# Moving a runtime loop ahead of the last sequence's normalisation in a fused attention and mixture-of-experts kernel

## The chip, the cores and the metric

The kernel runs on one core of one Trainium2 chip. Such a core has five engines that run side by side [...]: TensorE (PE in the profile; its weight loads are PEld), VectorE (DVE), ScalarE (ACT), GpSimd (POOL) and SyncE (SP), which here only issues transfers. Sixteen DMA engines move the data. The metric is device time in microseconds (us), the median of several runs; lower is better. Before the change the median of three runs is 1431.23 us (1428.58 to 1433.54).

## The reference

The input x holds 8 sequences of 512 rows of 256 numbers, all in float32. Two layers follow, each normalised on the way in and on the way out and added to its input:

```python
x = x + _layernorm(_L0_attn_ref(_layernorm(x, axis=-1), wq, bq, wkv, bkv, wo), axis=-1)
x = x + _layernorm(_L0_ffn_ref(_layernorm(x, axis=-1), gate_w, w_gate, w_up, w_down,
                               sh_gate, sh_up, sh_down), axis=-1)
```

The first is causal attention with 16 query heads of 128 that share 4 key and value heads, with a position code added to queries and keys. The second is a mixture of experts, plus a shared feed-forward part that every row passes:

```python
scores = jax.nn.softmax(logits, axis=-1)             # 64 experts
topk_w, topk_idx = jax.lax.top_k(scores, TOP_K)      # 6 of them for each row
...
pos = jnp.arange(T * TOP_K) - starts[eid_s]
valid = pos < CAP                                    # an expert takes its first 64 rows
...
y = jnp.einsum('tkh,tk->th', out_exp.reshape(T, TOP_K, H), topk_w)
y = y + gs * us @ sh_down.T                          # the shared part
```

T is here the 8 x 512 = 4096 rows of all sequences, so an expert's 64 places are filled in the order of the rows, and most experts are full long before the last rows come.

## The kernel before, in words

The kernel is written with a layer that places semaphores itself. For nearly the whole kernel the order of each engine's instructions is the order of the program text (a block that is opened with `tc.manual_schedule` for all five engines and closed with `order.close()`, L1015).

**Attention** goes through 8 x 16 heads in a software pipeline (the loop over k). The feed-forward steps of the sequence before are spread over the heads of the next, by a table of steps and places in `feed_forward`.

**Experts.** They are handled in 32 pairs. The first five sequences (`EARLY`) fill nearly all places; their rows are gathered, passed through the 32 pairs and scattered. Pairs that still have free places afterwards are listed in the tile `work`: its first number is the count of such pairs less one, and the numbers behind it name them. The first of these pairs, called "late", is worked out within the main order for sequences 5, 6 and 7: its weights are loaded beforehand, and each sequence gathers its rows by a product with a 0/1 matrix (`gather`), computes the pair (`gate_up`, `gate_up_hidden`, `turn_hidden`, `down`), and adds the result to its own sums with one more matmul in the PSUM banks of the sums.

**The other pairs** with free places, if there are any, are the business of the loop at L1019, `with tc.For_i(0, table["rest"], 1)`. Its count is only known on the chip. Its body reads back from device memory what the sequences 5, 6 and 7 left for it (scores and places in `lxg_d`, sums in `ly_d`, the rows x1 in `x1_d`), computes one pair, adds it to `ly_d`, normalises the rows again and writes them to the output again. In the kernel before, the loop is the last thing in the program. The trace holds no instruction of its body: with these inputs the count is zero. Every engine still goes through its gate, whose instructions carry the line L1019; the program's closing instructions carry L1094.

**The last part** (`last_part`, L837) is sequence 7's feed-forward, which has no further head to hide behind. In it,

- `other` and `output6` stand for sequence 6, whose feed-forward is finished here too. `output6()` advances the steps of `output` (L645): the first takes the statistics of the sums (VectorE, with a power on POOL), the second scales them (ACT) and adds x1 (POOL), the third issues the store of 512 KB to the output (SP, L655).
- `f` is the generator `shared` (L678) for sequence 7. It works through three chunks of the shared part; of the six steps, every second one is the hidden rows of a chunk, two VectorE instructions (L721, L722). The last `next(f)` is that of chunk 0.
- `l["part"](py, n)` adds the down product of chunk n to the sums `py` in two PSUM banks (L687), eight matmuls with their weight loads.
- the matmuls at L903 add the late pair's result, and then come sequence 7's statistics (`norm_scales`, L72), a copy of the sums by ACT that is stored to `ly_d` (L908, L909), subtraction of the mean (L911), the scaled sum with x1 (L913) and two stores of 256 KB to the output (L916).
- L872 stores sequence 7's x1 rows to `x1_d`. Only the loop's body would read these, as it would `ly_d`.

Of the kernel before, what the change touches and what calls it, by code (L numbers as in the profile page):

```python
# [16 lines left out]
ALU = mybir.AluOpType  # L17
AX = mybir.AxisListType

P = 128  # L20
B, T, E = 8, 512, 256
NT = B * T
NI = T // P
# [16 lines left out]
EARLY = 5  # L40
ET_ROWS = EARLY * T
# [3 lines left out]
def sandwich_kernel(ctx, tc, x, wq, bq_t, wkv, bk_t, bv, wo, gate_wt, w_gate, w_up, w_down,  # L45
                    sh_gate_t, sh_up_t, sh_down_t, pe_t, out):
    nc = tc.nc
# [14 lines left out]
    x1_d = dram.tile([NT, E], F32, tag="x1_d", name="x1_d")  # L62
# [3 lines left out]
    ly_d = dram.tile([NT - ET_ROWS, E], F32, tag="ly_d", name="ly_d")  # L66
# [5 lines left out]
    def norm_scales(tiles, name):  # L72

        n = len(tiles)
        st = small.tile([P, n, 6], F32, tag="st", name=f"st_{name}")
        for i in range(n):
            nc.vector.bn_stats(st[:, i, :], tiles[i])
        return scales_of(st, n, name)
# [23 lines left out]
    def rows_of(d, first):  # L102
        return d[first : first + T, :].rearrange("(i p) e -> p i e", p=P)
# [19 lines left out]
    with ExitStack() as part:  # L123
# [4 lines left out]
        p1 = pool("p1", 1)  # L128
        p2 = pool("p2", 2)
# [3 lines left out]
        ET = mybir.EngineType  # L133
# [28 lines left out]
        for half, (t, w) in enumerate(((sg_sb, sh_gate_t), (su_sb, sh_up_t))):  # L162
            nc.sync.dma_start(out=t[:, :, :FSH], in_=w.rearrange("(c p) n -> p c n", p=P))
            nc.sync.dma_start(out=t[:, :, FSH:],
                              in_=gate_wt.rearrange("(c p) n -> p c n", p=P)[:, :, ts(half, NX // 2)])
# [389 lines left out]
        def gate_up_hidden(key):  # L555
            l = pairs[key]
            pgu = l.pop("pgu")
            nc.vector.scalar_tensor_tensor(l["hid"], l["hid"], 1.0, pgu[:, 0, :], ALU.add, ALU.mult)
            nc.vector.scalar_tensor_tensor(l["hid"], l["hid"], 0.5, pgu[:, 1, :], ALU.mult, ALU.mult)

        def turn_hidden(key):
            l = pairs[key]
            pt = ps_s.tile([P, 2, P], F32, tag="s", name=f"pth_{key}")
            cols = l["hid"].rearrange("s (p c) -> s c p", c=2)
            for c in range(2):
                nc.tensor.transpose(pt[:FC, c, :], cols[:, c, :], ident)  # L566
            l["ht"] = p3.tile([FC, 2, P], F32, tag="ht", name=f"ht_{key}")
            on_dve(l["ht"], pt[:FC])
# [268 lines left out]
        def last_part(before, spare):  # L837


            b, xt, sums = B - 1, seqs[B - 1]["x"], po.pop(B - 1)  # L840
            l = {}
            other, shared6, output6 = before["l"], before["shared"], before["output"]
            for _ in spare:
                pass
            shared6()
            mv, rs = norm_scales([sums[i // 2][:, i % 2, :] for i in range(NI)], f"o{b}")
            next(other["f"])
            two = p2.tile([P, 2, NI * E], F32, tag="v", name="o_xt2")
            o, xt2 = two[:, 0].rearrange("p (i e) -> p i e", i=NI), two[:, 1].rearrange("p (c t) -> p c t", c=NC)
            st = small.tile([P, NI, 6], F32, tag="st", name=f"st_f{b}")  # L850

            for i in range(NI):
                nc.vector.scalar_tensor_tensor(xt[:, i, :], sums[i // 2][:, i % 2, :], rs[:, i : i + 1], xt[:, i, :],
                                               ALU.mult, ALU.add)
                nc.vector.bn_stats(st[:, i, :], xt[:, i, :])
            shift = shifts(mv, rs, f"o{b}")
            py6 = [ps_o.tile([P, 2, E], F32, tag=f"o{n}", name=f"py_{b - 1}_{n}") for n in range(2)]
            other["part"](py6, 2)
            mv, rs = scales_of(st, NI, f"f{b}")
            other["hidden"](0)  # L860
            fshift = shifts(mv, rs, f"f{b}")
            xg = p1.tile([P, NI, ROW], F32, tag="xg", name=f"xg_{b}")
            for i in range(NI):
                if i % 2:
                    scale_on_act(xg[:, i, :E], xt[:, i, :], rs, fshift, i)
                else:
                    normalize(xg[:, i, :E], xt[:, i, :], mv, rs, i)
            other["hidden"](1)
            transpose_rows(xt2, xg, f"f{b}")
            for i in range(NI):  # L870
                nc.gpsimd.tensor_scalar(xt[:, i, :], xt[:, i, :], shift[:, i : i + 1], 1.0, ALU.add, ALU.mult)
            nc.sync.dma_start(out=rows_of(x1_d, b * T), in_=xt)  # L872
            other["part"](py6, 0)
            f = shared(b, xt2, l, "msmsms")
            next(f)
            other["part"](py6, 1)
            r = route(b, xg, l)
            next(r)
            other["late"](py6)
            next(r)  # L880
            next(r)
            next(f)
            next(f)
            next(r)
            marked = marks(table["m"], xg[:, :, E:ROW], table["places"], b, p2, "xnt")
            next(f)
            next(f)
            gather("late", [(xg, marked[0])])
            gt = turn_scores(marked[1], b, p2, "kt", 5)
            gate_up("late")  # L890
            next(f)
            py = l["py"] = [ps_o.tile([P, 2, E], F32, tag=f"o{n}", name=f"py_{b}_{n}") for n in range(2)]
            l["part"](py, 2)
            l["part"](py, 1)
            gate_up_hidden("late")
            turn_hidden("late")
            l["part"](py, 0)
            down("late")
            output6()
            output6()  # L900
            output6()
            for i in range(NI):
                nc.tensor.matmul(py[i // 2][:, i % 2, :], lhsT=gt[:, ts(i, P)], rhs=pairs["late"]["dd"],  # L903
                                 start=False, stop=True, skip_group_check=True)
            mv, rs = norm_scales([py[i // 2][:, i % 2, :] for i in range(NI)], f"y{b}")
            y = p2.tile([P, NI, E], F32, tag="xnt", name=f"y_{b}")
            for n in range(2):
                nc.scalar.copy(y[:, ts(n, 2), :], py[n])  # L908
            nc.sync.dma_start(out=rows_of(ly_d, b * T - ET_ROWS), in_=y)  # L909
            for i in range(NI):  # L910
                nc.vector.tensor_scalar(o[:, i, :], py[i // 2][:, i % 2, :], mv[:, i, 0:1], None, ALU.subtract)  # L911
            for i in range(NI):
                nc.vector.scalar_tensor_tensor(xt[:, i, :], o[:, i, :], rs[:, i : i + 1], xt[:, i, :],  # L913
                                               ALU.mult, ALU.add)
                if i % 2:
                    nc.sync.dma_start(out=rows_of(out, b * T)[:, i - 1 : i + 1, :], in_=xt[:, i - 1 : i + 1, :])  # L916

        EARLY_TAGS = [(p3, "wgu"), (p3, "wd")]

# [91 lines left out]
        turned_at_once(NK - 1)  # L1011
        mix(NK - 1)
        project(NK - 1)
        last_part(behind, routed)
        order.close()  # L1015


# [1 line left out]
        with tc.For_i(0, table["rest"], 1) as n:  # L1019
            m = nc.values_load(table["work"][0:1, ds(n + 2, 1)], (ET.DVE, ET.SP), min_val=0, max_val=NM - 1)  # L1020
            pairs["late"] = {"m": m}
            load_gate_up("late")
            load_down("late")
            parts, gts = [], []
            for b in range(EARLY, B):
                q, tag = [(p1, "hid"), (p2, "v"), (p2, "v")][b - EARLY]
                xg = q.tile([P, NI, LROW], F32, tag=tag, name=f"rest_xg_{b}")
                nc.sync.dma_start(out=xg, in_=rows_of(lxg_d, b * T - ET_ROWS))
                q, tag = [(p1, "y"), (p2, "x"), (p2, "x")][b - EARLY]
                mark, marked = marks(m, xg[:, :, E:ROW], xg[:, :, ROW:], f"rest_{b}", q, tag)  # L1030
                parts.append((xg, mark))
                gts.append(turn_scores(marked, f"rest_{b}", p2, "kt", 5))
            gather("late", parts)
            gate_up("late")
            gate_up_hidden("late")
            turn_hidden("late")
            down("late")
            for b in range(EARLY, B):
                y = p2.tile([P, NI, E], F32, tag="xnt", name=f"rest_y_{b}")
                nc.sync.dma_start(out=y, in_=rows_of(ly_d, b * T - ET_ROWS))  # L1040
                for i in range(NI):
                    py = ps_m.tile([P, E], F32, tag="m", name=f"rest_py_{b}_{i}")
                    nc.tensor.matmul(py, lhsT=gts[b - EARLY][:, ts(i, P)], rhs=pairs["late"]["dd"], start=True, stop=True)
                    nc.vector.tensor_add(y[:, i, :], y[:, i, :], py)
                nc.sync.dma_start(out=rows_of(ly_d, b * T - ET_ROWS), in_=y)
                for _ in output(b, y, residual(b, p1, "xn")):
                    pass


# [48 lines left out]
```

## Time and profile before

| What | us |
|---|---|
| median of three runs | 1431.23 (1428.58 to 1433.54) |
| the profiled execution, its own time | 1433.63 |
| the profiled execution, span from first to last instruction | 1431.9 |
| PE busy in the span | 1393.9 |
| DVE busy | 888.9 |
| ACT busy | 505.3 |
| POOL busy | 428.9 |

The profile is that of one execution. Its page gives each engine's busy time, the share of every fortieth of the span, the DMA queues, the chain of work that ended last (followed back from the last instruction to whatever released it), and groups of instructions with the number of executions, the busy time and the mean duration. Waits, branches and the issue of transfers belong to an engine's sequencer (a q behind the engine's name) and aren't counted as busy. An L with a number is a line of the kernel, and a tile's name is that in the text without its number: `py` at L903 is `py_7`, the sums of sequence 7. Times within the trace are counted from the first instruction.

### The profile page before, as it was taken

To read this page: it belongs to the slowest core of one execution; us is meant where nothing else is said; L and a number is where in the kernel's file an instruction comes from. 1 tells how busy PE (TensorE), PEld (TensorE's weight loads), DVE (VectorE), ACT (ScalarE), POOL (GpSimd) and SP (SyncE) were. 2 spreads that over 40 slices of the span, in tenths; PEclk is the share of its full clock that TensorE was granted. 3 is DMA by queue.
4 is the path that set the end of the run, shared out by engine and by line. 5 is a ranking of instruction groups with operands and counts; after the bars stand their busy time and mean duration, and the time that the engine had idled before them with its cause. 6 is when DMAs were issued, how large, how long until landed. Compare 5 with 4: busy or idle time off the path is not lost.

```text
span 1431.9 us, 18567 instructions
## 1 busy us (share of the span) xinstructions
PE 1393.9 (97%) x5310; PEld 850.3 (59%) x5310; DVE 888.9 (62%) x3097; ACT 505.3 (35%) x1442; POOL 428.9 (30%) x686
## 2 busy tenths in 40 slices
PE   9999999999999999999999999999999999999895
PEld 5666665666656665656556665655556555556563
DVE  5565576656765576656765577566666545577634
ACT  2333333234422343234422343233443333444421
POOL 2231242113311232123211232124544344444311
PEclk9999999999999999999999999999999999999998
DMA  7765565356554564356544564358998789778702
GB/s 239 206 199 142 146 174 162 110 132 171 168 144 124 147 185 136 99 156 168 161 127 128 162 195 129 99 155 275 308 286 250 227 232 264 201 235 265 234 15 82
DMA packets 160791, 252.03 MB, mean 176 GB/s; under 512 B 16412, under 2 KB 136189, under 8 KB 160685
## 3 DMA queue, kind: packets, MB, share of 16 engines
q1 hardware_dynamic: 125869, 201.52, 48.4%
q10 hardware_dynamic: 28672, 39.85, 9.0%
q0 software_dynamic: 6144, 9.44, 3.3%
q8 instruction: 43, 0.70, 0.2%
q14 instruction: 63, 0.52, 0.1%
HBM read 143.01 MB, written 107.74 MB: 175 GB/s over the span
## 4 chain that ended last, share of the span: by engine, by line
PE 83%; DVE 8%; DMA 2%; ACT 2%; issue 2%; POOL 1%; SPq 0%; DVEq 0%; ACTq 0%; POOLq 0%
PE pav L349 17%; PE psc L289 16%; PE po L361 13%; PE pq L276 13%; PE pk L248 4%; PE pv L259 4%; PE psg L708 3%; PE psu L708 3%; PE pgu L549 2%; PE py L735 2%; DVE eb L322 2%; PE pd L575 2%; ACT e L296 2%; DMA ex_d<-eb 1%; PE pth L566 1%
## 5 line engine op out<-in xcount | busy, mean ns | idle before, releaser
L306 POOL TENSOR_SCALAR e<-e,recip 128x128 f32<-128x128 f32 x508 | 269.7, 571 | 775.3 <-DVE recip L303 762.4
L296 ACT ACTIVATE e<-e,least 128x128 f32<-128x128 f32 (+3 forms) x512 | 285.7, 559 | 350.4 <-DVE least L293 332.6
L289 PE MATMUL psc<-kt,qt 128*128 128x128 f32 (+3 forms) x1024 | 307.7, 438 | 9.9 <-DVE least L293 3.5
L349 PE MATMUL pav<-et,v 128*128 128x512 f32 (+3 forms) x1024 | 297.1, 433 | 1.4 <-DMA et<-ex_d 1.1
L349 PEld LDWEIGHTS pav<-et,v 128*128 128x128 f32 x1024 | 193.6, 190 | 161.0 <-issue 113.8
L293 DVE CUSTOM_DVE_ANT_0 e<-psc,mask 128x128 f32<-128x128 f32 (+3 forms) x512 | 232.2, 479 | 58.1 <-PE psc L289 52.2
L361 PE MATMUL po<-wo_sb,ao 128*128 128x256 f32 x1024 | 245.0, 383 | 0.7 <-ACT ao L109 0.7
L276 PE MATMUL pq<-xnt,wq_sb 128*128 128x512 f32 x512 | 240.9, 593 | 0.3 <-ACT sc L388 0.3
L361 PEld LDWEIGHTS po<-wo_sb,ao 128*128 128x128 f32 x1024 | 194.2, 191 | 72.5 <-issue 40.3
L109 ACT COPY ao<-pav 128x512 f32<-128x512 f32 x128 | 75.0, 586 | 435.8 <-PE pav L349 407.3
L322 DVE STREAM_TRANSPOSE eb<-e 128x128 f32<-128x128 f32 x756 | 227.5, 365 | 0.8 <-DMA ex_d<-eb 0.4
L289 PEld LDWEIGHTS psc<-kt,qt 128*128 128x128 f32 x1024 | 165.4, 190 | 85.3 <-DVE least L293 23.5
L279 DVE SCALAR_TENSOR_TENSOR qt<-pq,bq_sb,pe_sb 128x512 f32<-128x512 f32 x128 | 95.7, 748 | 106.0 <-PE pq L276 104.9
L276 PEld LDWEIGHTS pq<-xnt,wq_sb 128*128 128x128 f32 x512 | 95.9, 190 | 69.9 <-issue 64.0
L303 DVE RECIPROCAL recip<-total 128x4 f32<-128x4 f32 x128 | 22.8, 178 | 119.8 <-ACT e L296 119.8
L296 ACT ACTIVATION_READ_ACCUMULATOR e<-e,least 128x1 f32 x512 | 95.6, 187 | 0.0
L586 POOL DMA_INDIRECT y_d<-dd,idx x32 | 51.0, 1592 | 94.3 <-DMA y_d<-dd,idx 33.2
L248 PE MATMUL pk<-xnt,wkv_sb 128*128 128x512 f32 x128 | 60.3, 594 | 0.2 <-ACT xnt L109 0.2
L261 DVE TENSOR_TENSOR v<-pv,bv_sb 128x512 f32<-128x512 f32 x32 | 22.1, 691 | 60.8 <-PE pv L259 60.8
L259 PE MATMUL pv<-wkv_sb,xnt 128*128 128x512 f32 x128 | 59.1, 593 | 0.0
L251 DVE SCALAR_TENSOR_TENSOR kt<-pk,bk_sb,pe_sb 128x512 f32<-128x512 f32 x32 | 24.0, 750 | 47.5 <-PE pk L248 47.5
L112 DVE COPY ht<-pth 88x256 f32<-88x256 f32 x32 | 13.4, 418 | 55.2 <-PE pth L566 52.5
(197 smaller groups left out, 1113.6 us busy)
## 6 DMA issues: line engine op xcount, KB each, us to landing
ex_d<-eb SPq DMA_DIRECT2D x504, 160.0 KB
et<-ex_d SPq DMA_DIRECT2D x126, 640.0 KB
wgu<-in_w_gate ACTq DMA_DIRECT2D x32, 352.0 KB
wgu<-in_w_up ACTq DMA_DIRECT2D x32, 352.0 KB
wd<-in_w_down ACTq DMA_DIRECT2D x32, 352.0 KB
y<-y_d ACTq DMA_DIRECT2D x10, 512.0 KB
x<-in_x SPq DMA_DIRECT2D x8, 512.0 KB
x_d<-x SPq DMA_DIRECT2D x8, 512.0 KB
```

The lines of the kernel that those rows point to most:

```text
L248: nc.tensor.matmul(pk, lhsT=wkv_sb[:, c, g, 0, :], rhs=s["xnt"][:, c, :], start=c == 0, stop=c == NC - 1)
L259: nc.tensor.matmul(pv, lhsT=s["xnt"][:, c, ts(i, P)], rhs=wkv_sb[:, c, :, 1, :], start=c == 0, stop=c == NC - 1)
L276: nc.tensor.matmul(pq, lhsT=wq_sb[h // QPG][:, c, ts(h % QPG, D)], rhs=seqs[b]["xnt"][:, c, :], start=c == 0, stop=c == NC - 1)
L279: nc.vector.scalar_tensor_tensor(qt, pq, bq_sb[:, h : h + 1], pe_sb, ALU.add, ALU.add)
L289: nc.tensor.matmul(psc[:, :w], lhsT=l["qt"][:, ts(i, P)], rhs=seqs[b]["kt"][h // QPG][:, :w], start=True, stop=True)
L293: nc.vector.tensor_tensor_reduce(out=e, in0=psc[:, :w], in1=mask[:, T - w :], scale=-1.0 / math.sqrt(D), scalar=BIG, op0=ALU.add, op1=ALU. ...
L296: nc.scalar.activation(e, e, AF.Exp, bias=l["least"][:, i : i + 1], scale=-1.0, accum_out=l["total"][:, i : i + 1])
L306: engine.tensor_scalar(e, e, recip[:, n : n + 1], 1.0, ALU.mult, ALU.mult)
L322: nc.vector.transpose(blocks.rearrange("p c j t -> p j c t"), l["e"][i][:, js[0] * P : (js[-1] + 1) * P].rearrange("p (j c t) -> p j c t", ...
L349: nc.tensor.matmul(pav[:, :, j:, :], lhsT=seqs[b]["v"][:, j, ts(g, D)], rhs=l["et"][:, :, AT[j] : AT[j] + NI - j, :], start=j == 0, stop=j ...
L361: nc.tensor.matmul(po[b][i // 2][:, i % 2, :], lhsT=ao[:, ts(i, P)], rhs=wo_sb[:, h, :], start=h == 0 and i % 2 == 0, stop=h == NH - 1, sk ...
L708: nc.tensor.matmul(pp[:mw, :], lhsT=w_sb[:, c, ds(f0, mw)], rhs=xt2[:, c, :], start=c == 0, stop=c == NC - 1)
```

## The change

Three things are edited.

1. In `last_part`, sequence 6's three output steps, which stood together behind the last `down("late")`, are spread: the first behind `gate_up("late")`, the second behind `next(f)`, the third behind `l["part"](py, 0)`. The last `next(f)` moves from ahead of the products of chunks 2 and 1 to behind `gate_up_hidden`.
2. The loop moves ahead of the last rows' normalisation. `last_part` now ends with the matmuls at L903 and returns the sums in their banks and the x1 rows in their tile. The normalisation becomes a function of its own, `last_output`, called after the loop in a new block with a fixed order. The store of x1 (L872) and the copy and store of sequence 7's sums (L908, L909) go.
3. In the loop's body, sequence 7 is treated differently from 5 and 6: its share of a pair is added by matmuls to the banks that still hold its sums, and its rows aren't normalised there. One tile of the body changes its place (`x` becomes `xt2`).

```diff
-            nc.sync.dma_start(out=rows_of(x1_d, b * T), in_=xt)
             other["part"](py6, 0)
...
             gate_up("late")
-            next(f)
+            output6()
             py = l["py"] = [ps_o.tile([P, 2, E], F32, tag=f"o{n}", name=f"py_{b}_{n}") for n in range(2)]
             l["part"](py, 2)
             l["part"](py, 1)
             gate_up_hidden("late")
+            next(f)
+            output6()
             turn_hidden("late")
             l["part"](py, 0)
+            output6()
             down("late")
-            output6()
-            output6()
-            output6()
             for i in range(NI):
                 nc.tensor.matmul(py[i // 2][:, i % 2, :], lhsT=gt[:, ts(i, P)], rhs=pairs["late"]["dd"],
                                  start=False, stop=True, skip_group_check=True)
+            return py, xt
+
+        def last_output(py, x1):
+            b = B - 1
             mv, rs = norm_scales([py[i // 2][:, i % 2, :] for i in range(NI)], f"y{b}")
             y = p2.tile([P, NI, E], F32, tag="xnt", name=f"y_{b}")
-            for n in range(2):
-                nc.scalar.copy(y[:, ts(n, 2), :], py[n])
-            nc.sync.dma_start(out=rows_of(ly_d, b * T - ET_ROWS), in_=y)
-            for i in range(NI):
-                nc.vector.tensor_scalar(o[:, i, :], py[i // 2][:, i % 2, :], mv[:, i, 0:1], None, ALU.subtract)
-            for i in range(NI):
-                nc.vector.scalar_tensor_tensor(xt[:, i, :], o[:, i, :], rs[:, i : i + 1], xt[:, i, :],
-                                               ALU.mult, ALU.add)
+            for i in range(NI):
+                nc.vector.tensor_scalar(y[:, i, :], py[i // 2][:, i % 2, :], mv[:, i, 0:1], None, ALU.subtract)
+            for i in range(NI):
+                nc.vector.scalar_tensor_tensor(x1[:, i, :], y[:, i, :], rs[:, i : i + 1], x1[:, i, :], ALU.mult, ALU.add)
                 if i % 2:
-                    nc.sync.dma_start(out=rows_of(out, b * T)[:, i - 1 : i + 1, :], in_=xt[:, i - 1 : i + 1, :])
+                    nc.sync.dma_start(out=rows_of(out, b * T)[:, i - 1 : i + 1, :], in_=x1[:, i - 1 : i + 1, :])
...
-        last_part(behind, routed)
+        sums, x1_last = last_part(behind, routed)
         order.close()
...
-                q, tag = [(p1, "y"), (p2, "x"), (p2, "x")][b - EARLY]
+                q, tag = [(p1, "y"), (p2, "x"), (p1, "xt2")][b - EARLY]
...
-            for b in range(EARLY, B):
+            for i in range(NI):
+                nc.tensor.matmul(sums[i // 2][:, i % 2, :], lhsT=gts[-1][:, ts(i, P)], rhs=pairs["late"]["dd"],
+                                 start=False, stop=True, skip_group_check=True)
+            for b in range(EARLY, B - 1):
...
+        with tc.manual_schedule(engines={ET.PE, ET.DVE, ET.Activation, ET.Pool, ET.SP}):
+            last_output(sums, x1_last)
```

## The prediction

> **What bounds the kernel now.** I read the page first: the chain that ended last is TensorE for most of its length, so only what shortens the end of that chain can be gained. Then I asked for busy time in stretches of the last 47 us, because everything that the change touches lies there.
>
> ```profile
> span 1431.9 us, 18567 instructions
> PE 83%; DVE 8%; DMA 2%; ACT 2%; issue 2%; POOL 1%; SPq 0%; DVEq 0%; ACTq 0%; POOLq 0%
> ```
>
> ```profile
> 1396.00:1407.25 11.25, 11.07 (x59) 6.03 (x57) 9.38 (x31) 2.41 (x5) 0.00 (x0) 1.00 0.35 118
> 1407.25:1416.40 9.15, 8.61 (x42) 6.51 (x42) 3.81 (x16) 2.28 (x6) 1.92 (x3) 1.00 0.00 0
> 1416.40:1421.00 4.60, 0.00 (x0) 0.00 (x0) 4.41 (x15) 1.44 (x3) 2.84 (x4) 0.93 0.40 136
> 1421.00:1425.10 4.10, 0.00 (x0) 0.00 (x0) 0.00 (x0) 0.00 (x0) 0.00 (x0) 0.50 0.71 241
> 1425.10:1431.90 6.80, 0.00 (x0) 0.00 (x0) 0.00 (x0) 0.00 (x0) 0.00 (x0) 0.50 0.00 1
> ```
>
> The columns are stretch, its length, busy time of PE, PEld, DVE, ACT, POOL, then clock, DMA share, GB/s. TensorE is full until 1416.4; VectorE normalises the last sequence until 1421; DMA alone works until 1425.1; then nothing works for 6.8 us, and even DMA is silent. What fills them is in the view of the program's last line, for POOL, and of the loop's line, for SP and VectorE (duration min/median/max in ns, then first and last start):
>
> ```profile
> L1094 POOLq DRAIN  x3: 46/103/5302, 1425.7 to 1431.6; - x3
> L1019 SPq EVENT_SEMAPHORE  x21: 17/27/28, 1422.0 to 1426.6; - x21
> L1019 DVEq EVENT_SEMAPHORE  x14: 21/50/50, 1421.0 to 1425.5; - x14
> L1019 DVEq COMPARE_BRANCH  x3: 47/51/61, 1419.4 to 1425.6; - x3
> ```
>
> No instruction of the loop's body is in the trace: it runs zero times. But each engine executes its gate: a branch, a wait for its own work, then on leaving a dozen waits for all other engines and all DMA queues. The last of these is passed only when the last output rows have landed (1425.1), and only then, at 1425.7, does POOL reach the program's closing DRAIN, which takes 5.3 us. From its end to the end of the span are 0.8 us. So the chain ends: rows landed, gate 0.65, DRAIN 5.3, closing 0.8. The timeline shows the rows before that:
>
> ```profile
> 1415.50 1.62 DVE L77 BATCH_NORM_STATS2 st_y<-py 128x6 f32<-128x256 f32 x4 [0.77 <-PE py L903]
> ...
> 1417.52 1.65 DVE L911 TENSOR_SCALAR o_xt<-py,mv_y 128x256 f32<-128x256 f32 x4
> 1418.22 1.01 POOL L87 TENSOR_TENSOR rs_y<-ve_y,mhalf 128x4 f32<-128x4 f32 x1
> 1418.29 0.38 SPq L655 DMA_DIRECT2D out_dram<-x  x1
> 1418.71 0.51 SPq L909 DMA_DIRECT2D ly_d<-y  x1
> 1419.27 1.67 DVE L913 SCALAR_TENSOR_TENSOR x<-o_xt,rs_y,x 128x256 f32<-128x256 f32 x4
> 1420.18 1.62 SPq L916 DMA_DIRECT2D out_dram<-x  x2
> ```
>
> [...] Four engines here agree (7 to 17 ns), POOL's first does not: 5302 ns, against 170 ns for its DRAIN at the start of the program. [...] Here each engine's jump over the body took 0.4 to 0.6 us to its next instruction, with no instruction fetch inside it[...]. [...] from issue to last landing 128 KB of places took 1.95 us, 512 KB alone 2.9 to 3.0.
>
> **The change, part by part.**
>
> *Output of sequence 6, moved up between the PE blocks.* Its first step (four BATCH_NORM_STATS2, 1.39 us, aggregation and sum to 1.9) goes on VectorE from 1405.8 to 1407.65, right after the copy of gathered rows. Then the hidden rows of the pair (0.7, to 1408.4; their tanh is ready at 1407.62 anyway), and the last hidden chunk (1.4, to 1409.8), moved behind. Who waits for these? TensorE's transpose of the hidden rows at 1410.7 to 1410.9, after 3.65 us of py matmuls: 1.1 us of cover. That transpose also takes the bank that the moved chunk's second operand holds until 1409.8; same cover. If it were gone, TensorE would slip one to one. POOL's power runs at 1407.8 to 1408.8, VectorE's shift at 1409.8, ACT's four scalings (2.08) 1410.05 to 1412.1, ahead of ACT's copy of dd at 1413.9: 1.8 us of cover. POOL's four sums (2.77) end at 1413.5, and SP issues the 512 KB of output there instead of 1418.29; it lands 2.99 us later, at 1416.5 (as measured). TensorE keeps its end, 1416.35. Cost nothing.
>
> *Removed.* The store of x1 (512 KB at 1387, off every chain), two ACT copies of py (1.04) and the 512 KB store to ly_d. They are off VectorE's chain too, but DMA pays: before, three blocks drained back to back from 1419.3 to 1424, and the last 256 KB took 4.1 us from issue to landing.
>
> *The gate moved ahead of the last normalisation.* This is the cost. VectorE's first statistic needs only py, at 1415.5; now it needs every engine and landing. TensorE's own part is over at 1416.4. SP adds up eight DMA queues in order, 0.07 us each. Without the x1 store the early output sits on the first of these, landing at 1416.5, and VectorE follows with some eight more waits at 0.1 us, branch and start 0.3. Like before (landing 1425.07, three queues later VectorE past it at 1425.83), this gives a start at 1417.75. Were the landing a little earlier, TensorE is last and the start is 1416.85. The bounds are thus 1.35 and 2.25 us of delay[...]. I take 1.9, as the two releasers are within 0.15 us: start 1417.4. Behind it wait VectorE's 13 instructions, POOL's power and SP's two stores.
>
> *The last normalisation.* Before, 5.44 us from first statistic to last sum. The wait for the second py bank between statistics (0.18) is over by then; POOL's power no longer queues behind sums of sequence 6 (it started 0.6 us after its input), but the four subtractions (1.65) cover it in both. So 5.26: VectorE ends at 1422.66, SP issues at 1422.7, and 256 KB on a nearly idle queue land after about 2.3 us (an estimate between the 1.95 and 2.9 above): 1425.0. That is where it was: 1.9 lost at the gate, 2.0 regained.
>
> *The close.* POOL's last work is now its power, ending 3.1 us after the first statistic: 1420.5. Nothing stands between it and its closing DRAIN, which before carried no wait. At 5.3 us it runs 1420.6 to 1425.9, beside the last sums and stores, not after them. SP's closing wait passes at about 1425.4, so POOL's DRAIN is last, by half a microsecond. Plus 0.8: 1426.7. The sum: gate +1.9, bank wait -0.2, landing -1.8, gate at the end -0.65 with DRAIN hidden behind the landing -4.4 (of 5.3, 0.9 sticks out): -5.15 us in the profiled execution, whose span was 1431.9 and own time 1433.63 (1.7 lie around it). The median of the runs is 1431.23, 2.4 under that execution, a difference elsewhere; so 1431.23 - 5.15 = 1426.1. The DRAIN's length at its new place is not shown: from 0.17 to 5.3 us. At the short end SP's landing is last and the gain is 5.6, so only half a microsecond hangs on it. I take 5.3.
>
> **Rivals.**
> - *A fetch stall or late gate.* [...] sequence 6's rows land late. Each microsecond moves everything after. Against: no stall before. [...]
> - *The DRAIN stays last* (the slower side). If its 5.3 us wait for something at the program's end, or POOL must first wait for the last landing, then the gate is a loss with nothing to set against it but the shorter landing: 1425.0 + 0.65 + 5.3 + 0.8 = 1431.8, and with the gate's upper bound and a straggling DMA engine as before (the last 0.5 us of 1425.07) 1432.6. In the runs' terms 1431.1 to 1432.0, say 1431.6, slightly slower. It decides from a gate delay of 2 us on; over 0.3% slower needs over 6. For it: the length is unexplained. Against: before, DRAIN carried no wait and DMA was silent under it.
> - *The loop does run, or the edit does nothing*: same inputs, zero iterations before; hardly.
>
> **How the numbers follow.** Forecast 0.81, own range 1424.5 to 1427.7; fetch or gate 0.08; DRAIN last 0.10; rest 0.01. What a measurement of this kernel can tell from no change is about 0.3%, 4.3 us: below 1426.9 is faster, above 1435.5 slower. The forecast gives 0.75 of its 0.81 to faster, 0.06 to same; fetch or gate is same (0.08); DRAIN last 0.06 same, 0.04 slower, rest slower. Range 1423.4 to 1430.4: it holds the forecast with the runs' spread (2.5 us each way) and the stall, and leaves out most of DRAIN last.
>
> **What would show it.** VectorE's first statistic of py near 1417.4, behind the loop's waits; sequence 6's output issued near 1413.5; TensorE's end unmoved at 1416.4; no ly_d store there; POOL's long DRAIN starting some 0.1 us after its last power, not after the last landing; the end 0.8 us after it. Wrong if the DRAIN still starts or ends after the landing by 5 us, if TensorE's block slips, or if a jump takes over 1 us.

## The result and the profile after

The changed kernel takes 0.9972 of the time of the kernel before, with an interval of 0.9962 to 0.9983: some 4.0 us less (2.4 to 5.4). The medians of 22 runs each are 1429.98 and 1433.19 us, 3.2 us apart; the three runs from which the prediction reckoned lay 2 us under the longer series. The effect is clear of no change, and just short of the 0.3% that the prediction drew as its line.

The time went where the forecast had it go. Here are the stretches of the changed kernel that answer to those shown of before; the columns are again stretch, length, busy time of PE, PEld, DVE, ACT and POOL, clock, DMA share and GB/s. Everything up to the last sums runs 3.3 us later in this execution than in the profiled one of before, for reasons that lie earlier in the kernel (the copy of the late pair's rows starts at 1408.68 instead of 1405.37).

```profile
1410.56:1419.71 9.15, 8.62 (x44) 6.53 (x42) 2.76 (x10) 2.77 (x6) 3.78 (x5) 1.00 0.17 59
1419.71:1421.48 1.77, 0.00 (x0) 0.00 (x0) 0.00 (x0) 0.00 (x0) 0.00 (x0) 1.00 0.04 9
1421.48:1426.55 5.07, 0.00 (x0) 0.00 (x0) 5.01 (x17) 0.00 (x0) 1.02 (x1) 0.74 0.01 3
1426.55:1428.75 2.20, 0.00 (x0) 0.00 (x0) 0.00 (x0) 0.00 (x0) 0.00 (x0) 0.50 0.70 238
1428.75:1430.70 1.95, 0.00 (x0) 0.00 (x0) 0.00 (x0) 0.00 (x0) 0.00 (x0) 0.50 0.00 0
```

A new hole of 1.8 us has opened behind TensorE's end (1419.7), in which no engine works: the gate of the loop. The transfer behind the last sums has shrunk from 4.1 to 2.2 us, and the dead end, in which neither engines nor DMA work, from 6.8 to 1.95. The timeline shows the same in single steps (a bracket gives the engine's idle time before the instruction and what ended it), and the views of the loop's and of the closing instructions show who holds whom (durations in ns, then first and last start):

```profile
1416.63 0.38 SPq L655 DMA_DIRECT2D out_dram<-x  x1
...
1417.65 1.99 PE L902 MATMUL py<-dd_late,gt 128*128 128x256 f32 x8 [0.47 <-ACTq L1019]
1421.48 1.43 DVE L77 BATCH_NORM_STATS2 st_y<-py 128x6 f32<-128x256 f32 x4 [6.59 <-SPq L1019]
...
1423.30 1.65 DVE L911 TENSOR_SCALAR y<-py,mv_y 128x256 f32<-128x256 f32 x4
1423.47 1.02 POOL L87 TENSOR_TENSOR rs_y<-ve_y,mhalf 128x4 f32<-128x4 f32 x1 [6.87 <-DVE ve_y L85]
1424.87 1.66 DVE L913 SCALAR_TENSOR_TENSOR x<-y,rs_y,x 128x256 f32<-128x256 f32 x4
1425.77 1.16 SPq L915 DMA_DIRECT2D out_dram<-x  x2
```

```profile
L1019 DVEq EVENT_SEMAPHORE  x14: 21/50/50, 1414.9 to 1421.2; - x14
L1099 POOLq DRAIN  x3: 46/109/6380, 1423.4 to 1430.4; - x3
```

VectorE reached the gate at 1414.9 and left it at 1421.3. The bracket puts its release down to SP; wait by wait, VectorE passed the one for sequence 6's rows 0.06 us behind their landing (1419.98) and then walked through the rest of its gate. POOL's long DRAIN now starts at 1423.44, even a little ahead of the power that is POOL's last work, and its 6.38 us contain that power: from the power's end (1424.49) to the DRAIN's (1429.82) are again 5.3 us. So it now runs beside the last sums and their store instead of behind them. The chain view is of no help here: followed back from the end, it breaks off at the gate and gives VectorE's few instructions behind it as 0% of the span.

Single executions differ by several microseconds in the 1400 us ahead of the change. So all that follows compares the **tail**: the time from the start of VectorE's copy of the late pair's rows (the last `gxt_late`) to the end of the span. It is 26.49 us before (1405.37 to 1431.86) and 21.99 after: 4.50 less. Times "of the tail" below are counted from that start. Each tail is that of one profiled execution, but what the kernels have in common agrees closely: TensorE's last matmuls start 8.97 us into the tail in all eleven full-size kernels of this document.

| us of the tail | before | after |
|---|---|---|
| first statistic of the last sums | 10.14 | 12.80 |
| VectorE's last sum ends | 15.58 | 17.85 |
| POOL's last power ends | 13.87 | 15.81 |
| last rows landed | 19.71 | 20.02 |
| POOL's closing DRAIN ends | 25.66 | 21.13 |
| end | 26.49 | 21.99 |

### The profile page after: what moved, and what is told of

It is laid out like the page before. It is cut to its first block, busy times and chain, and to the rows that moved or that the text cites. A ratio compares the mean times of both kernels' runs of the same rounds, so it can differ in the third digit from the quotient of the medians.

```text
span 1430.7 us, 18562 instructions
## 1 busy us (share of the span) xinstructions
PE 1396.3 (98%) x5310; PEld 851.0 (59%) x5310; DVE 889.6 (62%) x3097; ACT 504.3 (35%) x1440; POOL 427.5 (30%) x686
## 3 DMA queue, kind: packets, MB, share of 16 engines
q0 software_dynamic: 6144, 9.44, 3.3%
```

## The experiments

The theory: the change gains by letting POOL's closing DRAIN, a fixed 5.3 us behind POOL's last work, run beside the last landing, and it pays for that with the gate ahead of the statistics. The rivals: the gain comes from the stores that were dropped or moved up; the DRAIN follows the program's end wherever that is; the gate costs little. A last question was what the DRAIN is at all. The ratios are all to the kernel before. Several rest on few runs (seven for the root on ACT, four each for the changed kernel without the loop and for the late store), so the changed kernels are told from each other by their tails.

**Taking the loop out of the kernel before.**

```diff
-        with tc.For_i(0, table["rest"], 1) as n:
-            ...
```

> The kernel before with the loop taken out (the work on other pairs with free places is left out; with these inputs there is none). Measure: the tail, from the start of VectorE's copy of the late pair's gathered rows to the end of the span; 26.5 us in the kernel before, 22.0 in the changed one. Theory (POOL's closing DRAIN is a fixed 5.3 us counted from POOL's last work, and the loop's gate only kept it from starting): the DRAIN runs from POOL's last power, 13.9 us into the tail, to 19.2; the rows land at 19.7, so the landing is last and the tail is 20.8 us, the time some 5.7 us under before. Rival (the DRAIN's length follows the end of the program, and the change gained by fewer and earlier stores): DRAIN still ends some 5 us after the landing, tail 25.5 to 26.

Tail 20.06 us, ratio 0.9958 (0.9945 to 0.997). All stores of before are still there, late as before, and yet the tail is 6.4 us shorter: the DRAIN's end, 5.3 us behind the power, comes at 19.18, and with it the landing at 18.92. The rival would have left 25.5.

```profile
L1062 POOLq DRAIN  x3: 46/113/6813, 1423.9 to 1431.3; - x3
```

So in the kernel before, the gate kept POOL from its DRAIN, and that made up most of the dead end of 6.8 us. The tail is 0.7 us shorter than expected, since the landing came at 18.92 and not at 19.71 as before. That difference seems to belong to the loop as well: in the kernel before, the records of the DMA packets have two instruction fetches of 8 KB beside the last three of these stores (1422.05 to 1422.36 and 1423.31 to 1423.62), whose last of sixteen parts landed 0.54, 0.42 and 0.78 us behind the fourteenth; without the loop there are no fetches until the rows have landed (more on this under the gate, below). That the fetches are the cause was not shown.

**The loop last again, all else as changed.**

```diff
-        with tc.For_i(0, table["rest"], 1) as n:
-            ...
         with tc.manual_schedule(engines={ET.PE, ET.DVE, ET.Activation, ET.Pool, ET.SP}):
             last_output(sums, x1_last)
+        with tc.For_i(0, table["rest"], 1) as n:
+            ...
```

> The changed kernel with the loop put back behind the last normalisation; the early output of sequence 6 and the two removed stores stay. Theory: no gate ahead of the statistics, so they start 10.1 us into the tail and the rows land at 17.4, but POOL reaches its DRAIN only through the gate behind the landing: 0.65 + 5.3 + 0.85, tail 24.2 us, about halfway between the two kernels. Rival (stores): all of the gain stays, tail 22.0 or less.

Tail 23.80, ratio 0.9981 (0.9968 to 0.9993). In this form the edits without the move give 2.7 of the 4.5 us.

```profile
L1100 POOLq DRAIN  x3: 46/103/5302, 1423.7 to 1429.6; - x3
```

One thing came out otherwise than meant: the second half of the last store slipped behind the gate and was issued at 18.77. The gate therefore waited only for the first half (landed at 16.76), and POOL's DRAIN ran from 17.66 to 22.96, 5.30 us, with nothing ahead of it but the gate. The last rows, landed at 20.89, were not last. With both halves ahead of the gate the tail would be some 24.4 us, 2.1 under before (an estimate: the second half landed at 17.57 in the kernel without the loop below, plus 0.65, 5.3 and 0.85). Neither of the plain stories, all stores or all move, fits; the sum does.

**POOL kept busy until the landing.**

```diff
             last_output(sums, x1_last)
+            nc.gpsimd.memset(x1_last[:, NI - 1, :], 0.0)
```

> The changed kernel with one more instruction on POOL: it clears a quarter of the last x1 tile, which it may only do once the last output store has read it and landed. Theory: POOL's DRAIN now starts only after the landing, 20.0 us into the tail; with the clearing 0.3, DRAIN 5.3 and close 0.85 the tail is 26.5 us and the whole gain is gone. Rival (stores; the DRAIN ends when the program does): tail 22.0 to 22.6.

Tail 26.59, ratio 0.9995 (0.998 to 1.001): the whole gain is gone, with gate, stores and order of everything else as in the changed kernel. The timeline and the closing instructions:

```profile
1427.29 0.31 POOL L1053 MEMSET x<- 128x256 f32 x1 [4.33 <-DMA out_dram<-x]
```

```profile
L1100 POOLq DRAIN  x3: 46/109/5648, 1427.3 to 1433.5; - x3
```

The clearing starts only when the store has landed, the DRAIN runs until 5.33 us behind the clearing (its 5.65 us contain it). This is the cleanest test of the theory: one instruction of 0.31 us costs 4.6 us, as the DRAIN ended 5.33 us behind POOL's last work and that now comes after the landing.

**POOL free of work behind the gate.** The root goes to ACT, the reciprocal to VectorE behind the subtractions.

```diff
-            mv, rs = norm_scales([py[i // 2][:, i % 2, :] for i in range(NI)], f"y{b}")
...
+            nc.vector.tensor_scalar_add(ve, mv[:, :, 1], EPS)
+            nc.scalar.activation(ve, ve, AF.Sqrt)
...
+            nc.vector.reciprocal(rs, ve)
```

> The changed kernel with the last inverse root taken off POOL: ACT takes the root, VectorE the reciprocal behind its four subtractions. POOL then has nothing to do behind the loop's gate. Theory: DRAIN runs from the gate's exit, 12.2 us into the tail, to 17.6, and the landing sets the end: VectorE's chain 0.2 longer by the reciprocal, landing at 20.2, close 1.1, tail 21.3 us, 0.7 less than the changed kernel. If ACT's table load is not hidden by the gate, up to 1.3 more. Rival (the DRAIN follows the end): tail 22.0 or more.

Tail 21.38, ratio 0.9958 (0.9942 to 0.9975). The DRAIN runs from the gate's exit, 12.41 to 17.71 of the tail, 5.30 us; the landing at 20.35 is last. ACT's table load takes 1.3 us and is hidden by VectorE's statistics.

```profile
L1109 POOLq DRAIN  x3: 46/103/5302, 1414.2 to 1422.9; - x3
```

This also shows that the DRAIN doesn't wait for the landing: here it has ended 2.6 us before it.

**The price of the gate where it now stands.** The changed kernel without the loop.

```diff
-        with tc.For_i(0, table["rest"], 1) as n:
-            ...
         with tc.manual_schedule(engines={ET.PE, ET.DVE, ET.Activation, ET.Pool, ET.SP}):
             last_output(sums, x1_last)
```

> The changed kernel without the loop (the work on other pairs is left out; with these inputs there is none). Prices the gate where it now stands. Theory (the gate holds the last statistics for 2.7 us and nothing else in the tail depends on it): the first statistic of the last sums starts 10.1 us into the tail, not 12.8, POOL's power ends at 13.4, its DRAIN at 18.8, tail 19.6 us against 22.0 in the changed kernel. Rival (the gate costs little, its waits only replace waits for TensorE): tail 21.5 to 22.0.

Tail 19.56, ratio 0.9936 (0.9919 to 0.9953). Without the gate VectorE takes the first statistic as soon as TensorE has made the first bank, 10.14 into the tail:

```profile
1416.67 1.46 PE L902 MATMUL py<-dd_late,gt 128*128 128x256 f32 x6
1417.30 1.63 DVE L77 BATCH_NORM_STATS2 st_y<-py 128x6 f32<-128x256 f32 x4 [3.93 <-PE py L902]
```

The gate delays the statistics by 2.66 us and the end by 2.43. It is the one price of the change that these traces show, and its size the term that the forecast had too small.

**What opens the gate.** Two kernels move the output of sequence 6, whose landing and TensorE's end were within 0.15 us in the forecast. The first puts the three steps back behind the down product:

```diff
             gate_up("late")
-            output6()
...
             next(f)
-            output6()
             turn_hidden("late")
             l["part"](py, 0)
-            output6()
             down("late")
+            output6()
+            output6()
+            output6()
```

> The changed kernel with sequence 6's three output steps back together behind the late pair's down product; the loop stays ahead of the last normalisation. Theory (the gate opens on the landing of sequence 6's rows): they are issued 12.9 us into the tail and land at 15.9, the statistics follow 1.5 later at 17.4, POOL's power ends at 20.4, DRAIN at 25.7, tail 26.6 us: the early output is what makes the move pay. Rival (TensorE's end opens the gate): tail stays at 22.

Tail 26.97, ratio 1.0 (0.9988 to 1.0011). Sequence 6's rows are issued at 12.92 of the tail, land at 16.28, and the statistics start at 17.79:

```profile
1421.59 0.38 SPq L655 DMA_DIRECT2D out_dram<-x  x1
1426.46 1.43 DVE L77 BATCH_NORM_STATS2 st_y<-py 128x6 f32<-128x256 f32 x4 [8.42 <-SPq L1019]
```

Moving the loop without the early output gains nothing: what the DRAIN gives, the late gate takes.

The second leaves the steps where the change put them, but issues the store behind the loop:

```diff
             l["part"](py, 0)
-            output6()
             down("late")
...
-            return py, xt
+            return py, xt, output6
...
+            store6()
             last_output(sums, x1_last)
```

> The changed kernel with only the store of sequence 6's rows moved, from ahead of the loop to behind it (in the loop's body one tile takes another place, as that of sequence 6's rows is still in use). Theory (the landing of these rows holds the gate): now TensorE's last matmul at 11.0 us of the tail opens it, the statistics start at 11.4, POOL's power ends at 14.4, DRAIN at 19.8, tail 20.6 us, 1.4 less than the changed kernel. Rival (the series of waits in each engine's gate sets the start, whatever lands last): statistics at 12.6 or later, tail 21.8 or more.

Tail 20.53, ratio 0.9948 (0.9927 to 0.9968).

```profile
1419.63 0.38 SPq L655 DMA_DIRECT2D out_dram<-x  x1
1419.65 1.43 DVE L77 BATCH_NORM_STATS2 st_y<-py 128x6 f32<-128x256 f32 x4 [5.13 <-PEq L1018]
```

Now TensorE's own gate instructions release VectorE (in the changed kernel it was SP), at 11.35 of the tail instead of 12.80. The series of waits is then mostly walked through beforehand: the statistics start 0.38 us behind TensorE's last matmul, where they start 1.5 behind the landing in the changed kernel.

**Both improvements together:** the two edits above, the root on ACT and the store behind the loop, in one kernel.

> Both: sequence 6's store behind the loop, and the last inverse root taken by ACT and VectorE so that POOL has no work behind the gate. Theory: statistics at 11.5 us of the tail, VectorE done at 16.8, rows landed at 19.0, POOL's DRAIN long over, tail 20.1 us; by the runs 6.4 us under the kernel before, some 0.45%. Rival (gate set by its series of waits): tail 21.3 as with the root alone.

Tail 19.80, ratio 0.9955 (0.9937 to 0.9972), against 0.9972 for the changed kernel. It is the shortest tail of a kernel with all of its work. The intervals overlap, also with that of the late store alone (0.9948), so it is by the tail, not by the runs, that it is told from the others.

**What the DRAIN is.** Three small kernels leave out attention and the experts. They copy the input to the output and do one power on POOL last; where there are gathers, the power waits for the last of them to land.

```diff
+    for n in range(64):      # none, 1 or 64 gathers of 128 rows
...
+        nc.gpsimd.indirect_dma_start(out=g, out_offset=None, in_=x[:, :],
+                                     in_offset=bass.IndirectOffsetOnAxis(ap=idx[:, 0:1], axis=0))
...
```

> A small kernel that only copies the input to the output through SBUF, with one inverse power on POOL as its last work there; all of attention and the experts is left out. No transfer is issued by POOL. It asks what the closing DRAIN on POOL is. Theory (it belongs to the transfers that POOL issued, of which the kernel before has 64): DRAIN takes about 0.2 us, as at the start of the program. Rival (POOL's closing DRAIN costs 5.3 us in any program): 5.3 us.

> The same small kernel with one gather of 128 rows issued by POOL ahead of everything else; attention and experts are left out. Theory (software transfers make DRAIN long, by a fixed amount): 5.3 us behind POOL's last work. If the cost grows with their number: well under 1 us. Rival (any program): 5.3 us here and without the gather.

> The same small kernel with 64 gathers of 128 rows issued by POOL, as many transfers as the kernel before issues there; attention and experts are left out. Theory, fixed amount: 5.3 us, as with one. If the cost grows with their number: 5.3 us here and a small part of it with one. Rival (any program): 5.3 us in all three.

The closing DRAINs of the three, in this order (one run and one profile each; the longest of each three contains the power, 1.02 to 1.05 us, that is still under way when it starts):

```profile
L117 POOLq DRAIN  x3: 34/76/1116, 29.0 to 33.8; - x3
```

```profile
L117 POOLq DRAIN  x3: 34/101/1242, 28.8 to 33.6; - x3
```

```profile
L117 POOLq DRAIN  x3: 40/101/6398, 107.3 to 114.2; - x3
```

Behind the power's end the DRAIN lasts 0.07 us without transfers issued by POOL, 0.16 with one, and 5.32 with 64, the number that the kernel has (32 gathers and 32 scatters). So it is not a fixed price of a program's end: it comes with the transfers that POOL issued, and is larger with 64 than with one, by about 0.08 us for each more on average. Whether it grows in a straight line was not tried. Each transfer, here and in the kernel, is one of 128 rows, so transfers and rows aren't told apart; DMA packets are, as the kernel's 64 transfers made 6144 of them and the 64 here 3072, with the same 5.3 us.

**Paying it early.** If it is a debt of these transfers, it can be paid at any time after them. In the kernel before, POOL is idle for 26 us in the last part.

```diff
             gather("late", [(xg, marked[0])])
+            nc.gpsimd.drain()
             gt = turn_scores(marked[1], b, p2, "kt", 5)
```

> The kernel before, loop last, nothing moved; one line added: a DRAIN on POOL behind the late gather of sequence 7, where POOL is idle for 26 us. Theory (what DRAIN takes 5.3 us for is left over from the 64 transfers that POOL issued, and can be paid at any time after them): the added DRAIN takes 5.3 us there without holding anything up, the closing one about 0.1 us, tail 26.5 - 5.2 = 21.3 us, as good as the changed kernel without moving the loop. Rival (the closing DRAIN is long wherever the program ends): both take 5.3 us, tail 26.5.

Tail 22.32, ratio 0.9978 (0.9967 to 0.9989). The added DRAIN and the closing ones:

```profile
L889 POOLq DRAIN  x1: 6507/6507/6507, 1390.3 to 1390.3; - x1
```

```profile
L1095 POOLq DRAIN  x3: 34/49/103, 1430.3 to 1431.9; - x3
```

The added one lasts until 5.33 us behind the four instructions on the x1 rows (L871) that POOL was at, and holds nothing up; the closing one takes 0.05 us. One line gains 4.17 us of the tail, nearly as much as the whole change. I had expected 21.3; the missing microsecond is SP, whose own walk through the gate ends 1.7 us behind the landing and had been hidden by the DRAIN.

## Why the prediction was right, and where it was not

**Sequence 6's output moved up, at no cost: right.** TensorE's last matmuls start 8.97 us into the tail in both kernels; the moved chunk of hidden rows ends at 1413.0, 0.84 us ahead of the transpose that needs it (forecast 1.1). The store is issued 7.95 into the tail, forecast 8.1.

**The gate, 1.9 us from bounds of 1.35 and 2.25: too small.** It measured 2.66, outside the bounds. This is the step that was mis-sized. The lower bound is sound (the kernel with the late store: 11.35 into the tail, 1.21 of delay), but "I take 1.9" placed the start between two releasers as if they shared it, where the later one decides. Two things went beyond the upper bound, though the store was issued 0.18 us earlier than forecast: it took 3.35 us to land instead of 2.99 (fifteen of its sixteen parts had landed 3.1 us after the issue, the last one 0.3 later), and the walk from landing to first statistic took 1.50 us instead of 1.25.

For the late part the records of the DMA packets suggest a cause. They have fetches of instructions, 8 or 16 KB each, while the engines go through the gate: five from 1418.20 to 1422.89 in the changed kernel, five from 1417.49 to 1426.90 in the kernel before. Of the 36 stores in the eleven tails, 21 had no such fetch beside them, and the last of their sixteen parts landed at most 0.08 us behind the fourteenth. Of the 15 that had one, 12 had their last part 0.41 to 1.44 us behind (0.44 here, with fetches of 8 KB at 1418.20 and 1419.23). The prediction's "no instruction fetch inside it" doesn't hold to the letter either: in the kernel before, one of 16 KB (1417.5 to 1418.5) runs over ACT's jump. It held nothing up there: ACT's next instruction came 0.40 us behind the jump's end, and 0.42 in the changed kernel, where no fetch runs at that jump.

In the walk, VectorE stood still for 0.42 us between its last two waits, where 0.05 is usual. It did so at this same place in all six kernels that have the loop ahead of the normalisation. In the kernels with the loop last it didn't, but there its jump over the body took 0.52 us to the next instruction, against 0.17 here. So a stop of this size seems to have been in the gate before, at the jump, where nothing waited for it, and the changed program has it at another place. In all six a fetch of instructions begins 0.67 us after it (1421.19 and 1421.87 in the changed kernel); with the late output none runs during it. What VectorE waits for there was not shown.

**The last normalisation, 5.26: nearly right.** 5.05 us. The wait for the second bank fell away as forecast (the four statistics take 1.43 us instead of 1.62). The rest lies where the forecast put nothing, at POOL's power: before, it ended 0.06 us behind the subtractions and held the first sum up by 0.18; in the changed kernel it ends 0.46 ahead of them. The kernel without the loop, which has the bank wait and not this one, takes 5.25. (Behind the gate are 17 instructions of VectorE, not 13.)

**The landing, 2.3: right**, 2.14 us for 256 KB on a nearly idle queue.

**The DRAIN beside the landing, from 5.3 us to 0.9 that stick out: right** (1.1 stuck out), and the premise with it: nothing stood between POOL's last power and its DRAIN, and 5.3 us pass behind POOL's last work, or behind its arrival at the DRAIN where the gate brings it there later (5.30 to 5.33 in all eleven kernels that do the full computation or leave only the loop out; with the early DRAIN, in that one). The detail that the DRAIN would start 0.1 us behind the power was wrong: its record starts when the sequencer gets there (1423.44, the power's at 1423.47), and only its end tells.

**The sum.** Forecast -5.15 in the profiled tail, measured -4.50. POOL's path sets the end, and on it the gate took 0.76 us more, while the rest gave 0.1 back (from statistics to power's end 3.01 for 3.1, the DRAIN's end 5.32 later for 5.4, the close 0.86 for 0.8). The median came out 3.9 us above the forecast: 2.0 of them lie in the three runs that it reckoned from, 0.65 in the tail, and the rest is within the spread of the runs. The median lies inside the stated range by 0.4 us and outside the forecast's own range of 1424.5 to 1427.7; taken off the three runs that the forecast started from, the measured 4.0 us would have given 1427.2, inside both. The likeliest case, faster by over 0.3%, was not met: 4.0 us, or 4.5 by the tail, are at that line and not clear of it.

**Rivals.** The DRAIN staying last is excluded (it ends at 21.13, not 25.7), and what it would have given was made by hand with the clearing: 26.59, the same as before, as the working had it. A late gate is real: 0.4 us beyond the upper bound came, and without the early output it takes everything. A fetch stall, an estimate of the author's, was not: no engine's jump over the loop's body took over 0.6 us to its next instruction. That fetches cost the changed kernel some tenths in the ways above is likely, but not shown.

## What to carry to other kernels

Look at the end of the profile for time in which neither engines nor DMA work, and ask which sequencer instruction fills it and what it had to wait for: 5.3 us here that no view counted as busy. A runtime loop was paid for here even though it ran zero times (2.66 us at the statistics), since its gate gathers every engine and every landing; put it where the landings ahead of it are old, and issue nothing just before it that can wait until after (one store moved behind it, and the statistics started 1.45 us earlier). If POOL issues as many transfers as here (64, and a DRAIN of 5.3 us), let it be through with its work early or drain it in an idle stretch (4.17 us of the tail for one line), and look afterwards for what had been hidden behind it.

## What the runs showed of the hardware

- POOL's DRAIN took 0.07, 0.16 and 5.32 us behind POOL's last work with 0, 1 and 64 transfers issued by POOL, in the large kernel 130 us or more after the last of them had landed, in the small one with 64 gathers 1.4 us after.
- That cost could be paid once, early: 5.33 us at 1390 to 1397, then 0.05 at the end.
- A loop gate with zero iterations in the middle of a chain delayed the next instruction by 2.66 us and the end by 2.43. Of the 2.66, 1.5 lie behind the landing that came last: nine waits of VectorE at 0.1 us each, one per pair of semaphores, a stop of 0.42, branch and start. SP's waits took 0.07 us each.
- 256 KB from SBUF to device memory on a nearly idle queue landed 2.14 us after the issue began, and 3.3 to 4.1 us after it with 1.25 MB of other stores just ahead (4.10 in the kernel before).
- Stores of 256 or 512 KB with an instruction fetch of 8 or 16 KB beside them had their last part 0.41 to 1.44 us behind the fourteenth in 12 of 15 cases, those without one at most 0.08 in 21. That the one causes the other was not shown.
